# Weight sums in one list at a higher rate, and the down product's first quarter sums begun when their tile is written

## The chip, the cores and the metric

The kernel runs on one core of a Trainium2 chip. The metric is the device time of one execution in microseconds (us); lower is better. Each kernel is timed in several runs and the median is told. One execution is also recorded by the profiler. All data are float32.

## The reference

The input is 2048 tokens of 512 features. A first layer (time mixing and channel mixing as in RWKV) and a gated feed-forward layer are added to it, one after the other:

```
h = layer_norm(layernorm(x));  hh = time_shift(h)
k, v, r = three 512x512 products of mixtures of h and hh
x1 = layernorm(x) + (sigmoid(r) * wkv(k, v)) @ Wo.T
kv = silu(mix(ln(x1)) @ Wkey.T) @ Wval.T          # 512 -> 2048 -> 512
x  = x + x1 + sigmoid(mix(ln(x1)) @ Wcr.T) * kv
gate, up = split(layernorm(x) @ w_gate_up.T)      # 512 -> 2 x 2048
out = x + (silu(gate) * up) @ w_down.T            # 2048 -> 512
```

## The kernel before

**Tiling.** The tokens are cut into four blocks of 512 (`NB` = 4). The first half of the program takes all blocks through the first layer, the second half takes them through the feed-forward layer. Each 512x512 product is done in seven products of 256x256 quarters instead of eight (Strassen in Winograd's form). That needs sums of quarters on both sides. The sums of activations (`sums_of`, line 435) are made block by block on VectorE. The sums of weights don't depend on a block: each is made once, stored in DRAM scratch, and then loaded like a weight.

**Weight sums** (`prepare`, line 140). One job loads four quarters on GpSimd's DMA queue into `raw` tiles, forms four sums on VectorE (128x512, line 155) and stores each on GpSimd's queue. The jobs are in a queue, `preps`. The first nine are pushed at the start. `WK, WR, WV, WO` follow before the loop over blocks. The last nineteen, the list `late`, are the feed-forward layer's: eight for gate and up, and eleven for the down product, four of them (`d`) feeding three later ones (`dd`). They are pushed within block 1, after `up_unit(1, 0)`. A job can begin only when it is pushed; with depth 1, the next begins when the one ahead has ended.

**Pacing.** After each product, `tick` (line 287) adds `credit[1]` to a credit, and as long as a planner's slack of VectorE time is positive, a step of the head job may be taken for one credit (`prep_one`). A step goes ahead of the background work (norms, mixes). After a job's loads, five ticks pass before its first sum (`WAIT`). `credit[1]` is 0.5 until the nineteen are pushed, then 0.42. What is left at the end of the first half is forced out in one go, before the first half's pools are given back:

```python
1283    while preps:
1284        need_sums(preps[-1][0])
1285    mixes.close()
1286    last_room()
```

PE, VectorE and ScalarE run their instructions in the order in which this code issues them.

**Down product** (`down_product`, line 1075). In the second half, the product with `w_down` goes down one level more: each of the seven products (`DOWN`, line 1037) is again seven products of 128x128 quarters, its steps `first` to `seventh`. The quarter sums of the activation tile, four VectorE instructions into `quads` tiles (`quarter_sums`, line 1064), are asked for per product n. For n = 0 (tile `B11`) and n = 1 (tile `B22`) this is done in `done` of the last up unit (line 1020), behind the four sums of the hidden tile itself. `done` is put off by two ticks. For n > 1 they are asked for when product n - 2 ends. If the third product of n finds its sums not asked for, it runs the put-off functions, then all urgent work ahead of them (`product`, line 1118). The two last products of the up unit (`held`) are interleaved with the first steps of n = 0. For blocks 0 to 2 the next block's gate unit is computed between the up unit and the down product; the last block has none.

Of the kernel before, what the change touches and what calls it, by code (L numbers as in the profile page):

```python
# [33 lines left out]
WK, WV, WR, WO, WCR = range(5)  # L34
# [15 lines left out]
B11, B12, B21, B22, T1, T2, T4 = range(7)  # L50
# [8 lines left out]
def rwkv_ffn_kernel(  # L59
# [80 lines left out]
    def prepare(n, own):  # L140

        raw = []
        for k in range(4):
            t = prep.tile([P, 2, HB], F32, tag="raw", name="raw") if own else q_tile("q")
            paced(nc.gpsimd.dma_start(flat(t), sources[n][k]))
            raw.append(t)
        yield 1
        a11, a12, a22, a21 = raw
        for k, o, i0, i1, op in (
            (0, a22, a21, a22, ALU.add),  # L150
            (2, a21, a11, a21, ALU.subtract),
            (1, a11, a22, a11, ALU.subtract),
            (3, a12, a12, a11, ALU.subtract),
        ):
            tt(o, i0, i1, op)
            nc.gpsimd.dma_start(sums[n][k], flat(o))  # L156
            yield
# [24 lines left out]
    def load_x(b, queues=None):  # L182
        t = tok_tile("x")
        for k in range(NT):
            eng = queues[k] if queues else nc.sync
            paced(eng.dma_start(t[:, k, :], x_t[b][:, k, :]))
        return t
# [55 lines left out]
    credit = [0.0, 0.0]  # L243
# [17 lines left out]
    def begin(item):  # L261
        if not item[4]:
            item[4] = True
            next(item[2])
            item[1] = WAIT

    def prepare_all(ns, own, depth):
        empty = not preps
        for n in ns:
            preps.append([n, 0, prepare(n, own), depth, False])  # L270
        if empty:
            for item in list(preps)[:depth]:
                begin(item)
# [31 lines left out]
    def push(name, gen, ready=None):  # L305
        background.append([ready, gen, name, False, background])

    def urgent(name, gen):
        hot.append([None, gen, name, False, hot])

    def need(name):
        while name not in finished:
            run_one(True)
        slack[0] = min(slack[0], 0.0)
        spent[0] = 0.0
# [46 lines left out]
    def tt(out, a, b, op):  # L362
        nc.vector.tensor_tensor(out, a, b, op)  # L363
        cost(size(out))
# [70 lines left out]
    def sums_of(B):  # L435

        for o, i0, i1 in (T1, B12, B11), (T2, B22, T1), (T4, B21, T2), (T3, B22, B12):
            tt(B[o], B[i0], B[i1], ALU.subtract)
            yield
# [272 lines left out]
    def time_norm(b):  # L712
        xb = xin.pop(b)
        mv = small.tile([P, NT, 2], F32, tag="mv", name="mv")
        yield from moments(xb, mv)
        var = small.tile([P, 2 * NT], F32, tag="var2", name="var2")
        affine(var, mv)
        two = small.tile([P, 2 * NT], F32, tag="two", name="two")
        yield from rsqrt(var, two, 2 * NT)
        rstd, both = two[:, :NT], two[:, NT:]  # L720
        h = tok_tile("h")
        yield from scaled(xb, h, mv, both)
        hT = htp.tile([P, NC, TB + 1], F32, tag="hT", name="hT_a")
        hTs[b, "a"] = hT
        tails[b] = residual(b, xb, [(mv[:, t, 0:1], rstd[:, t : t + 1]) for t in range(NT)])
        yield 1
        yield from shifted_norm("a", h, hT, LN1G, LN1B)
# [89 lines left out]
    def time_mix(b, name):  # L817
        row = {"k": MK, "r": MR, "v": MV}[name]
        yield from mix((b, name), hTs[b, "a"], row, b < PLAIN)

    def push_mix(b, name, gen):
        norm = f"normb{b}" if name in ("cr", "ck") else f"norm{b}"
        push((b, name, "t"), gen, lambda: norm in finished and op_free())
# [42 lines left out]
    def v_unit(b):  # L866
        q = qs[b]

        def sink(i, j, c):
            tt(q[i, j], c, q[i, j], ALU.mult)  # L870

        def done():
            hidden_sums((b, "g"), q, b < PLAIN)

        product_of(b, WV, "v", sink, False, done)
# [4 lines left out]
    def out_unit(b):  # L880
        need(("x1", b))

        def sink(i, j, c):
            v = block_view(x1s[b], i, j)
            tt(v, c, v, ALU.add)

        product_of(b, WO, "g", sink, True, free=None)
# [20 lines left out]
    def channel_mix(b, name):  # L908
        yield from mix((b, name), hTs[b, "b"], {"cr": CR, "ck": CK}[name])

    def gate_unit(b):
        def sink(i, j, c):
            s = q_tile("sr")
            nc.scalar.activation(s, c, AF.Tanh, scale=0.5)  # L914
            gates[b, i, j] = s

        product_of(b, WCR, "cr", sink, True)

    def up_unit(b, g):
        s = {}  # L920

        def sink(i, j, c):
            t = q_tile("s")
            nc.scalar.activation(t, c, AF.Silu)
            s[i, j] = t

        unit(
            [WKEY + g],
            [Lazy((b, "ck"))],
            sink,  # L930
            False,
            lambda: hidden_sums((b, g), s),
            op_done if g == 3 else None,
        )
# [27 lines left out]
    def load_resid(b):  # L962
        r = tok_tile("resid")
        paced(nc.sync.dma_start(r, resid[b]))
        loads[b] = r, load_x(b)
# [42 lines left out]
    def ffn_up(b, g):  # L1008
        s = gated.pop((b, g))
        hid = hidden.setdefault(b, {})  # L1010

        def sink(i, j, c):
            q = (B11, B12, B21, B22)[2 * i + j]
            if q not in hid:
                hid[q] = hidden_tile()
            tt(hid[q][:, g], c, s[i, j], ALU.mult)
            if g == 3:
                made.add((b, q))

        def done():  # L1020
            if g == 0:
                for t in (T1, T2, T4):
                    hid[t] = hidden_tile()
            urgent((b, "f", g), sums_of({t: hid[t][:, g] for t in hid}))
            if g == 3:
                made.update((b, t) for t in (T1, T2, T4, "T3"))
                for n in range(2):
                    quarter_sums(b, n)

        unit([WU + g], [Lazy((b, "z"))], sink, False, done, op_done if g == 3 else None)  # L1030

# [7 lines left out]
    def hidden_tile():  # L1039
        return room["hidden"].tile([P, 4, 2, HB], F32, tag="hid", name="hid")  # L1040
# [15 lines left out]
    def quarter_operand(b, n):  # L1056

        x = quarters(hidden[b][DOWN[n][1]])
        new = room["sets"][n % 2]
        x[T1], x[T2], x[T4] = new[:3]  # L1060
        x["T3"] = new[3] if n < 2 else x[B12]
        return x

    def quarter_sums(b, n):
        x = quarter_operand(b, n)
        asked.add((b, n))

        def run():
            for o, i0, i1 in (T1, B12, B11), (T2, B22, T1), (T4, B21, T2), ("T3", B22, B12):
                tt(x[o], x[i0], x[i1], ALU.subtract)  # L1070
                yield

        urgent((b, "quarters", n), run())
# [144 lines left out]
    late = [n + g for g in range(4) for n in (WG, WU)] + [("dd", A11)]  # L1218
# [25 lines left out]
    push_mix(0, "ck", channel_mix(0, "ck"))  # L1244
    r_unit(1)
    v_unit(1)
    prepare_all((WK, WR, WV, WO), True, 1)
    for b in range(NB):
        nxt = b + 2 < NB
        if nxt:  # L1250
            xin[b + 2] = load_x(b + 2)
        if b == NB - 1:
            load_resid(0)
        gate_unit(b)
        if b + 1 < NB:
            out_unit(b + 1)
        need((b, "ck"))
        if nxt:
            push(f"norm{b + 2}", time_norm(b + 2))
        for g in range(4):  # L1260
            up_unit(b, g)
            if b == 1 and g == 0:
                prepare_all(late, True, 1)
                credit[1] = 0.42
            if g == 0:
                if nxt:
                    push_mix(b + 2, "k", time_mix(b + 2, "k"))
                    push_residual(b + 2)
                    push_mix(b + 2, "r", time_mix(b + 2, "r"))
                if b + 1 < NB:  # L1270
                    push(f"normb{b + 1}", channel_norm(b + 1))
                if nxt:
                    push_mix(b + 2, "v", time_mix(b + 2, "v"))
                if b + 1 < NB:
                    push_mix(b + 1, "cr", channel_mix(b + 1, "cr"))
                    push_mix(b + 1, "ck", channel_mix(b + 1, "ck"))
        if b == NB - 1:
            push((0, "z", "t"), ffn_in(0), op_free)
        down_unit(b)
        if nxt:  # L1280
            for n, u in (("k", k_unit), ("r", r_unit), ("v", v_unit)):
                u(b + 2)
# [90 lines left out]
```

## Time and profile before

| | |
|---|---|
| median of 3 runs | 1298.44 us (1295.93 to 1301.96) |
| the profiled execution's own time | 1300.73 us |
| its span, first to last instruction | 1298.6 us, so 2.1 us lie around it |
| PE matmuls | 1245.6 us busy (96% of the span) |
| PE weight loads | 1114.2 us (86%), beside the matmuls |
| VectorE (DVE) | 777.6 us (60%) |
| ScalarE (ACT) | 368.5 us (28%) |
| GpSimd (POOL) | 151.4 us (12%) |
| DMA | 288.55 MB, mean 222 GB/s |
| mean granted TensorE clock | 0.984 |

In the profile, a line such as L527 is the kernel's source line. L527 is the matmul of the seven-product units, L640 that of the plain units, L1126 that of the down product, L414 a transpose. L363 is every VectorE two-input operation, so the tile names tell them apart: `raw` is a weight sum, `quads` a quarter sum, `hid<-hid` a sum of the hidden tile, `u` and `s` a combination of products. L145 and L156 are the loads and stores of a weight sum. A float32 matmul has two records.

### The profile page before, as it was taken

Reading aid. Unit: us, or ns where it says so; the run is one execution under the profiler, and the core shown is the slowest. Engines: PE = TensorE matmul, PEld = TensorE weight load, DVE = VectorE, ACT = ScalarE, POOL = GpSimd, SP = SyncE. Lnnn points to the kernel's source line nnn. Section 1 sums busy time; section 2 is a strip of 40 time slices with the busy share of each in tenths; the row PEclk is TensorE's granted clock in tenths of the full one; section 3 lists DMA queues with packets and bytes.
Section 4 is the critical chain, followed back from the end, with each engine's and each line's share of the span. In section 5 each row is a group of like instructions: output and inputs, shape, how many; then the busy total and the mean of one; then the engine's idle time right before and its main releaser. Section 6 shows DMA issues by size and latency. Waiting matters only on the chain.

```text
span 1298.6 us, 18324 instructions
## 1 busy us (share of the span) xinstructions
PE 1245.6 (96%) x6572; PEld 1114.2 (86%) x6572; DVE 777.6 (60%) x1416; ACT 368.5 (28%) x687; POOL 151.4 (12%) x276
## 2 busy tenths in 40 slices
PE   9999999999999999999992999999999999999988
PEld 7888888878888788888881788998889988998878
DVE  4757587576774767544743365665756564663456
ACT  5533352343522424113100223212221222112211
POOL 2222221200111111121213000000000000000000
PEclk9999999999999999999996899999999999999989
DMA  5666777865778777788777654795459854785556
GB/s 191 223 211 235 238 237 256 289 197 180 231 221 257 240 231 238 243 305 284 239 240 266 212 153 146 219 330 190 146 163 295 280 154 145 240 280 154 154 172 202
DMA packets 137960, 288.55 MB, mean 222 GB/s; under 512 B 17296, under 2 KB 18320, under 8 KB 136848
## 3 DMA queue, kind: packets, MB, share of 16 engines
q1 hardware_dynamic: 115424, 215.53, 53.3%
q0 software_dynamic: 21440, 70.27, 15.1%
q10 hardware_dynamic: 1008, 1.59, 0.3%
q8 instruction: 53, 0.87, 0.3%
q14 instruction: 35, 0.29, 0.1%
HBM read 245.39 MB, written 41.94 MB: 221 GB/s over the span
## 4 chain that ended last, share of the span: by engine, by line
PE 89%; DVE 3%; ACT 3%; DMA 2%; issue 2%; POOL 1%; POOLq 0%; DVEq 0%
PE ps L527 68%; PE ps L1126 13%; PE ps L640 6%; PE ps L414 1%; DMA dd<-raw 1%; DMA raw<-in_wd 1%; DVE u L363 1%; ACT mix L465 1%; DVE hid L363 1%; POOL dd L156 0%; ACT r L835 0%; DVE quads L363 0%; DMA raw<-d 0%; DMA x<-in_x 0%; ACT e L840 0%
## 5 line engine op out<-in xcount | busy, mean ns | idle before, releaser
L527 PE MATMUL ps<-zT,w 128*128 128x256 f32 x1792 | 393.7, 381 | 28.5 <-ACT u L544 28.5
L527 PEld LDWEIGHTS ps<-zT,w 128*128 128x128 f32 x1792 | 340.0, 191 | 74.9 <-ACT u L544 28.9
L527 PE MATMUL ps<-mix,w 128*128 128x256 f32 x1232 | 273.5, 381 | 5.3 <-ACT s L544 5.3
L527 PEld LDWEIGHTS ps<-mix,w 128*128 128x128 f32 x1232 | 234.8, 191 | 38.3 <-ACT s L544 6.1
L363 DVE TENSOR_TENSOR u<-ps,u 128x512 f32<-128x512 f32 x128 | 88.5, 691 | 167.2 <-PE ps L527 164.9
L544 ACT COPY u<-ps 128x512 f32<-128x512 f32 x128 | 74.8, 584 | 327.0 <-PE ps L527 327.0
L527 PE MATMUL ps<-w,s 128*128 128x256 f32 x512 | 114.3, 379 | 0.0
L527 PEld LDWEIGHTS ps<-w,s 128*128 128x128 f32 x512 | 97.0, 190 | 13.0
L1126 PE MATMUL ps<-w,hid 128*128 128x128 f32 x832 | 105.9, 277 | 0.4 <-ACT r L1138 0.4
L1126 PEld LDWEIGHTS ps<-w,hid 128*128 128x128 f32 x832 | 100.8, 194 | 1.1 <-ACT r L1138 0.5
L1126 PE MATMUL ps<-w,quads 128*128 128x128 f32 x704 | 91.6, 280 | 8.2 <-issue 5.5
L527 PE MATMUL ps<-w,t 128*128 128x256 f32 x432 | 96.3, 379 | 1.7 <-ACT sr L914 1.2
L1126 PEld LDWEIGHTS ps<-w,quads 128*128 128x128 f32 x704 | 85.6, 195 | 10.7 <-issue 5.9
L527 PEld LDWEIGHTS ps<-w,t 128*128 128x128 f32 x432 | 81.9, 190 | 13.5 <-ACT sr L914 1.6
L363 DVE TENSOR_TENSOR raw<-raw 128x512 f32<-128x512 f32 x92 | 63.2, 687 | 45.1 <-DMA raw<-in_wd 20.4
L640 PE MATMUL ps<-mix,w 128*128 128x256 f32 x384 | 85.5, 385 | 1.1 <-DVE mix L371 1.1
L640 PEld LDWEIGHTS ps<-mix,w 128*128 128x128 f32 x384 | 73.7, 193 | 11.6 <-DVE mix L371 1.5
L363 DVE TENSOR_TENSOR s<-ps,s 128x512 f32<-128x512 f32 x64 | 44.1, 690 | 59.5 <-PE ps L527 45.7
L363 DVE TENSOR_TENSOR u<-u,u 128x512 f32<-128x512 f32 x64 | 44.1, 689 | 59.4 <-ACT u L544 59.4
L1138 ACT COPY r<-ps 128x128 f32<-128x128 f32 x112 | 29.7, 265 | 151.2 <-PE ps L1126 151.2
L1208 POOL DMA_DIRECT2D out<-resid x12 | 8.6, 717 | 440.8 <-DVE resid L363 440.8
L363 DVE TENSOR_TENSOR hid<-hid 128x512 f32<-128x512 f32 x84 | 56.6, 687 | 1.1
(127 smaller groups left out, 1177.7 us busy)
## 6 DMA issues: line engine op xcount, KB each, us to landing
w<-sum SPq DMA_DIRECT2D x304, 256.0 KB, 3.2
w<-in_w SPq DMA_DIRECT2D x256, 256.0 KB, 3.3
w<-dd SPq DMA_DIRECT2D x112, 256.0 KB, 3.6
raw<-in_w POOLq DMA_DIRECT2D x48, 256.0 KB, 4.8
sum<-raw POOLq DMA_DIRECT2D x48, 256.0 KB, 3.9
w<-d SPq DMA_DIRECT2D x48, 256.0 KB, 3.4
q<-in_w POOLq DMA_DIRECT2D x36, 256.0 KB, 5.4
sum<-q POOLq DMA_DIRECT2D x36, 256.0 KB, 3.5
```

Of the source, the lines that this page charges most:

```text
L363: nc.vector.tensor_tensor(out, a, b, op)
L414: nc.tensor.transpose(flat[:, t * P : (t + 1) * P], h[:, t, c * P : (c + 1) * P], ident)
L465: nc.scalar.activation(dst(c), hT[:, c, 0:TB].rearrange("p (j t) -> p j t", j=2), AF.Copy, scale=onem[:, row - MK, c : c + 1],)
L527: mm = nc.tensor.matmul(pz[:, m, :], lhsT=lhsT, rhs=rhs, start=first and g == 0 and m == 0 and k == 0, stop=g == last and k == 1, skip_gro ...
L544: nc.scalar.copy(tmp[name], acc["z"])
L640: mm = nc.tensor.matmul(acc[i, j][:, m, :], lhsT=act[:, k, lo] if by_token else wg[:, k, lo], rhs=wg[:, k, :] if by_token else act[:, k, : ...
L1126: mm = nc.tensor.matmul(dst, lhsT=x[k][:, g, :], rhs=wt[:, g, :], start=first and g == 0, stop=g == 3, skip_group_check=True,)
L1138: nc.scalar.copy(st["r"][:, m, n * P : (n + 1) * P], st["z"])
L1208: eng.dma_start(out_t[b][:, 2 * j : 2 * j + 2, i * HB : (i + 1) * HB], rs[b][:, 2 * j : 2 * j + 2, i * HB : (i + 1) * HB],)
```

## The change

The nineteen late jobs join the list of four before the loop, so that they can begin as soon as those four have ended. The rate after `up_unit(1, 0)` becomes 0.55 in place of 0.42. The quarter sums for n = 0 and n = 1 are asked for as soon as the last up unit has written that tile's last quarter (`B11`, `B22`), no longer in `done`.

```diff
@@ ffn_up, sink
             if g == 3:
                 made.add((b, q))
+                if q in (B11, B22):
+                    quarter_sums(b, 0 if q == B11 else 1)
@@ ffn_up, done
                 made.update((b, t) for t in (T1, T2, T4, "T3"))
-                for n in range(2):
-                    quarter_sums(b, n)
@@
-    prepare_all((WK, WR, WV, WO), True, 1)
+    prepare_all([WK, WR, WV, WO] + late, True, 1)
@@
             up_unit(b, g)
             if b == 1 and g == 0:
-                prepare_all(late, True, 1)
-                credit[1] = 0.42
+                credit[1] = 0.55
```

## The prediction

> **What bounds the kernel now.** I read the page's first two parts, then PE's waits, then the chain of waits and the timeline around the two longest, then windows. On the page PE is busy in nearly every fortieth of the span, 1245.6 of 1298.6 us. So TensorE sets the time, and what can be won is its idle time and its time at a lowered clock.
>
> ```profile
> PE   9999999999999999999992999999999999999988
> ...
> PEclk9999999999999999999996899999999999999989
> ```
>
> Slice 22 of 40 is the exception: PE at 2 tenths, then a lowered clock. The last slices are short too. PE's waits name them (us in total, times, longest):
>
> ```profile
> PE ps L527 <- ACT u L544: 28.5, 1, 28.5
> PE ps L1126 <- issue: 5.5, 1, 5.5
> PE ps L527 <- ACT s L544: 5.3, 2, 3.0
> PE ps L1126 <- DVE quads L363: 2.0, 3, 0.7
> ```
>
> One wait of 28.5 us is more than half of all idle time. It is put down to a ScalarE copy, but the chain shows what that copy stood behind (start, us, what):
>
> ```profile
> 684.86 8.61 DMA dd<-raw
> ...
> 699.04 4.05 DMA raw<-d
> ...
> 707.52 4.85 DMA raw<-in_wd x2
> ...
> 712.45 0.70 DVE raw L363
> ...
> 715.24 0.69 DVE s L363
> 715.95 0.63 ACT s L1003
> 716.58 0.48 ACT u L544
> 717.11 62.96 PE ps L527 x281
> ```
>
> These are the last weight sums, forced out by line 1284. VectorE's first combination of the second half (`s`) stands behind them, ScalarE behind that, PE behind ScalarE. The 5.5 us wait is in the last block's down product (start, us):
>
> ```profile
> 1243.77 2.74 DVE L363 TENSOR_TENSOR hid<-hid 128x512 f32<-128x512 f32 x4
> 1246.42 0.68 DVE L363 TENSOR_TENSOR quads<-hid 128x512 f32<-128x512 f32 x1
> 1247.14 1.42 DVE L363 TENSOR_TENSOR quads<-hid,quads 128x512 f32<-128x512 f32 x2
> ...
> 1247.93 2.05 PE L1126 MATMUL ps<-w,quads 128*128 128x128 f32 x8 [5.54 <-issue]
> ```
>
> PE is done at 1242.4. The third product of n = 0 needs `quads`, and VectorE makes them only after the add of 1242.43, one `hid` and four sums of `hid`. The three waits of 0.67 us on `quads` (825.7, 969.4, 1113.1) are the same place in blocks 0 to 2, where another unit covers most of it.
>
> **Part 1, the wait between the halves.** The changed program has the same instructions; only their order differs. In VectorE's order before, fourteen weight sums stand directly ahead of that first combination. After, the last weight sum stands ahead of the four `zT` sums and fifteen more instructions. Those `zT` sums ran at 655.4, and PE reached the seam at 681.5. So the jobs end some 26 us before they would hold anything up. **Gain 28.5.** Next late: PE did four products from 681.52 to 688.6, and the fifth needs the `u` copy. In the timeline that is add at about 685 (0.69), `s` on ScalarE (0.63), copy (0.57), the copy no earlier than the third product's end at about 686.9: done by 687.5, ahead of 688.6. The new pools' memory was last read by the down product's `sr` operations (to 683.9 on VectorE, same queue). SP issues the same list in the same order; the residual's load behind the store of 684.20 (median 9.1 us to landing) could hold it until 693.3, with weights loaded ahead. I take 0 for the seam, upper end 3.
>
> The clock: between 688.6 and 717 the granted clock falls to 0.59, is 0.50 to 720 and 0.87 to 725. 98 weight loads then took 23.24 us; at the pace before the stall (32 records in 6.91 us from 660.80 to 667.71, 0.216 each) they take 21.2. **Gain 2.1.** The Trainium skill, "TensorE: Matmul & The Clock Gate", What's actually happening, says that the clock halves after an idle window of about 3.4 us and returns after as long a busy one. An estimate by it is 1.7 us lost at each of the two long stalls, and the sum below would be 1.5 smaller. The trace agrees on the half clock but not on the threshold: 2.31 us of idling at 270 brought 0.50, 2.97 us at 436 left 1.00.
>
> **Part 2, quarter sums.** In the last block `B11` is whole at 1230.86 and VectorE then idles until 1235.27 (4.42 us): room for four sums (2.8). The third product then starts at 1242.4. **Gain 5.5.** Next late is n = 1: its four sums follow `B22` (whole at 1240.34) and end near 1243.2; its third product comes six products of 0.89 us after 1242.4, at 1247.8. They delay the add of 1242.43, hence `hid` and its sums, to 1247.3; `T2`, second of those, is ready at 1245.9 and needed near 1251. The sums of n = 2 start near 1249.0, `T2`'s quarter is out at 1250.4 and needed near 1255. No wait is left by this count, with 3 to 5 us of cover each. If none of it came, 8.3 would be lost to me. The clock again: five products took 1247.93 to 1255.24, 7.3 us, at 0.50 to 0.71; at 0.89 (1255.24 to 1257.92, three products) they take 4.5. **Gain 2.8.** Blocks 0 to 2: 0.67 on `quads` and 0.28 on the copy behind them, 0.95 each. **Gain 2.9.**
>
> **Part 3, what the jobs do where they go.** No DMA or sum is added. GpSimd's 28 issues and VectorE's 16 sums of 674 to 717 are spread forward. The row for `raw` in windows by time (DVE busy, POOL busy, clock, DMA share, GB/s):
>
> ```profile
> 255.00:307.00 52.00, 2.74 (x4) 2.17 (x4) 0.97 0.63 200
> 307.00:674.00 367.00, 41.19 (x60) 67.38 (x124) 1.00 0.77 246
> 674.00:717.00 43.00, 11.06 (x16) 15.23 (x28) 0.73 0.76 266
> ```
>
> After, 76 sums (52.2 us) lie in about 270 to 655, 0.136 of VectorE in place of 0.112; VectorE as a whole was busy 225.4 of 367. The eight that fall into 255 to 307 bring it from 35.2 to about 40 of 52. GpSimd's transfers go from 88 to 104 GB/s, so DMA from 246 to about 261, share 0.82. PE never waited on a weight in the trace, and the same loads lead by the same ring of 12. Both loads fit on average; what counts is places where PE waits on VectorE. At 296.78 PE waited 0.50 for a `t` sum; in the new order `t`'s first sum no longer runs ahead of the add before it: +0.7. At 436.44 it waited 2.97 behind, among others, two of `mix` (1.42 together) that now follow instead: -1.6 with the gap between them. The 2.31 at 270 is ahead of any difference and stays. Take a gain of 0.9; bounds: the rest of the 2.97 gone too (gain 2.3), or one landing wait of a load at such a place (the longest in the trace was 6.7, most of it covered; loss 3).
>
> **The sum.** 28.5 + 2.1 + 5.5 + 2.8 + 2.9 + 0.9 = 42.7. From the profiled execution, 1300.73 - 42.7 = 1258.0. It lies 2.3 above the median, so by the median 1255.7; I say **1256**.
>
> **Rivals.**
> 1. *Another wait takes the seam* (residual load, pool memory, a late copy). 3 us beyond the count and the clock loss kept (2.1): near 1261. Against it: every other releaser there is done by 688. 0.08.
> 2. *The last block's stall only moves*, since one VectorE queue does `hid` sums, eight quarter sums and `r` adds between 1240 and 1252: 5.5 + 2.8 stay, 1264. For it: VectorE is busy without a break in 1242 to 1248. Against: the cover counted above. 0.08.
> 3. *Slower: the forced wait is paid in nineteen pieces.* A job's first sum stands in VectorE's queue whether or not its loads have landed; PE's adds queue behind. In 255 to 670 it waited so for 6.67, 4.37 and 3.62 us, with no PE wait; the two longer were in block 2's down product, where VectorE has little to do. In single-weight units a product is 1.72 us and about two are ahead: 6.67 each time would idle PE 3.2 us, 19 times 61, and the time 1317. It decides from 42.7 / 19 = 2.2 us per job, that is a landing wait of 5.7 in every job. Against: loads land in 4.2 us (median, 8.4 at most), five ticks are 8.6, the 3.62 fell among single-weight units and was covered, and the other waits put down to such a load are at most 1.33 (one of 5.57 has no named releaser). [...] 0.04.
> 4. *The same in part*: about 1 us at each job, 1256 + 19 = 1275. 0.06.
> That the change doesn't do what it says is excluded for part 1 by the order; for part 2 it is rival 2.
>
> **How the numbers follow.** The forecast holds 0.74. Its own range is 1255.7 less 2.3 and 2.5 (lowest run shown against the median), and plus 3.9 and 3.5 (highest): 1251 to 1263. With rivals 1 and 2 the range is **1250 to 1268**; it leaves out 3 and 4. About 0.5% (6.5 us) is what a measurement of this kernel can tell from no change. All cases but 3 are faster by more than that: faster 0.95, same 0.01, slower 0.04.
>
> **What would show it.** PE's wait `<- ACT u L544` of 28.5 gone, no `raw` operation after the `zT` sums, PEclk without the 6 and 8; the `quads` of the last block near 1231 less the shift, the 5.5 and three 0.67 gone; PE's idle sum near 15 in place of 53. Wrong if PE waits on `u`, `s` or `mix` whose VectorE queue shows a wait on `DMA raw`, or if a wait on weights (`DMA w`) appears.

## The result, and the profile after

The changed kernel takes **1258.24 us** (median of 4 runs, 1257.87 to 1260.03) beside 1299.22 us for the kernel before in the same rounds (1295.93 to 1301.96): ratio **0.9688, 95% interval 0.9663 to 0.9713**. In five more rounds it took 1257.19 (1256.22 to 1260.08) beside 1299.59: ratio 0.9681 (0.9666 to 0.9697). The forecast was 1256.

The profiled execution took 1260.03 us, its span is 1258.2. First the page, the same two rows as before (40 slices in tenths):

```profile
PE   9999999999999999999999999999999999999998
...
PEclk9999999999999999999999999999999999999999
```

The slice with a 2 is gone, and so are the 6 and the 8 of the clock. PE is busy 1240.0 of 1258.2 us, so it idles 18.2 us where it idled 53.0; the prediction had said near 15. The largest of PE's waits that are left (us in total, times, longest):

```profile
PE ps L527 <- ACT s L544: 6.0, 3, 2.3
PE ps L527 <- issue: 1.8, 1, 1.8
```

The waits of 28.5 on `u`, of 5.5 in the last down product and the three on `quads` are not there any more. But `<- ACT s L544` has grown from two waits to three: one of them the prediction did not have.

The timeline at the seam between the halves (start, us, engine, line):

```profile
683.97 46.35 PE L527 MATMUL ps<-zT,w 128*128 128x256 f32 x214
```

That is 214 matmul records in a row without a gap. VectorE's queue in front of it:

```profile
653.70 0.68 DVE L363 TENSOR_TENSOR raw<-raw 128x512 f32<-128x512 f32 x1
658.06 0.69 DVE L363 TENSOR_TENSOR zT<-zT 128x512 f32<-128x512 f32 x1 [3.69 <-ACT zT L987]
...
687.70 0.69 DVE L363 TENSOR_TENSOR s<-ps,s 128x512 f32<-128x512 f32 x1 [1.38 <-PE ps L527]
```

The last weight sum ends at 654.4, ahead of the `zT` sums and 29.6 us before PE reaches the seam. The first combination `s` now waits for PE, no longer PE for it. The `u` copy follows from 689.35 to 689.93, and PE's fifth product would need it at about 691.0 (683.97 and four products of 1.77).

The last block's down product, VectorE first, then PE:

```profile
1199.06 0.69 DVE L363 TENSOR_TENSOR quads<-hid 128x512 f32<-128x512 f32 x1
...
1201.12 0.68 DVE L363 TENSOR_TENSOR quads<-hid 128x512 f32<-128x512 f32 x1
...
1212.55 2.74 DVE L363 TENSOR_TENSOR hid<-hid 128x512 f32<-128x512 f32 x4
```

```profile
1210.40 1.05 PE L1126 MATMUL ps<-w,quads 128*128 128x128 f32 x8
```

The four quarter sums of n = 0 end at 1201.8, in VectorE's gap, and no longer behind the four sums of `hid`. The third product starts on time at 1210.40, right behind the one ahead of it, and the next ones follow every 0.89 us (1211.30, 1212.19, 1213.08), the pace that the kernel before has only from 1254.35 on.

**Where the 40.4 us of span went.** The same marks are read from both timelines: PE's start after its first wait in the first half (270.15 before, 268.29 after), its arrival at the seam (681.52, 683.97), the first L1126 product of block 0 (819.42, 791.05) and of block 3 (1236.73, 1204.90), and the first of the two waits on `r` near the end (1291.50, 1251.12).

| stretch | before | after | gain | predicted |
|---|---|---|---|---|
| start to the first mark | 270.15 | 268.29 | 1.86 | 0 |
| to the seam | 411.37 | 415.68 | -4.31 | 0.9 |
| seam to block 0's down product | 137.90 | 107.08 | 30.82 | 30.6 |
| to block 3's down product | 417.31 | 413.85 | 3.46 | 2.9 |
| to the mark before the end | 54.77 | 46.22 | 8.55 | 8.3 |
| rest | 7.10 | 7.08 | 0.02 | 0 |

Everything behind the seam came as predicted, to 1.1 us in 42. The first half did not. The 1.86 at the start are not the change's, which alters nothing so early: the granted clock of the first 20 us was 0.91 in the one execution and 1.00 in the other.

**The first half.** PE's waits in the first half after the change (end of each row: idle time before it, and its releaser):

```profile
268.29 8.86 PE L527 MATMUL ps<-mix,w 128*128 128x256 f32 x32 [2.31 <-ACT s L544]
295.64 1.96 PE L527 MATMUL ps<-w,t 128*128 128x256 f32 x8 [1.23 <-ACT sr L914]
434.27 7.17 PE L527 MATMUL ps<-mix,w 128*128 128x256 f32 x32 [1.67 <-ACT s L544]
460.55 1.97 PE L527 MATMUL ps<-w,t 128*128 128x256 f32 x8 [1.83 <-issue]
512.95 8.86 PE L527 MATMUL ps<-mix,w 128*128 128x256 f32 x32 [2.06 <-ACT s L544]
```

Before, these places had 2.31, 0.50, 2.97, 1.23 and nothing. So +0.7 and -1.3 are the two terms that the prediction had (+0.7, -1.6); +0.6 near 460 and 2.1 at 512.95 were not in it. The last is paid twice: its 32 records take 8.86 us in place of 7.17, since the granted clock is 0.65 from 512.9 to 517. That adds 1.7. Together that is a loss of 3.8; some 0.5 of the 4.3 is not placed.

What releases PE at 512.95 stands in ScalarE's queue:

```profile
505.35 2.55 ACT L465 ACTIVATE mix<-hT_b,onem 128x512 f32<-128x512 f32 x4
...
507.80 0.56 ACT L544 COPY u<-ps 128x512 f32<-128x512 f32 x1
508.26 1.33 ACT L465 ACTIVATE mix<-hT_b,onem 128x512 f32<-128x512 f32 x2
...
512.33 0.57 ACT L544 COPY s<-ps 128x512 f32<-128x512 f32 x1
```

Four `mix` operations stand ahead of a copy out of PSUM (`ps` in the rows, where the matmuls write), and two more, with their VectorE halves, ahead of the combination that the last copy waits for. Before, the same place looked like this:

```profile
506.91 1.32 ACT L465 ACTIVATE mix<-hT_b,onem 128x512 f32<-128x512 f32 x2
508.14 0.56 ACT L544 COPY u<-ps 128x512 f32<-128x512 f32 x1
```

There, four `mix` had run earlier, from 502.66 to 505.2, and ScalarE idled for 1.16 after them. Two stand directly ahead of the copy, and none between it and the next copy (511.49). They are block 3's channel mixes, background work that the planner deals out. After the change they come later, and so does the end of the transposes that they follow: before, PE makes this block's 16 transpose records in one go at 493.27, after it 12 at 491.70 and the last 4 only at 501.65. The change touches no line of all this; it only gave other ticks to the weight sums.

### The profile page after: what moved, and what is told of

It is laid out like the page before. It is cut to its first block, busy times and chain, and to the rows that moved or that the text cites. A ratio compares the mean times of both kernels' runs of the same rounds, so it can differ in the third digit from the quotient of the medians.

```text
span 1258.2 us, 18321 instructions
## 1 busy us (share of the span) xinstructions
PE 1240.0 (99%) x6572; PEld 1110.7 (88%) x6572; DVE 777.4 (62%) x1416; ACT 369.0 (29%) x687; POOL 151.3 (12%) x276
## 4 chain that ended last, share of the span: by engine, by line
PE 93%; ACT 3%; DVE 2%; DMA 1%; issue 1%; POOL 0%; DVEq 0%
PE ps L527 71%; PE ps L1126 14%; PE ps L640 6%; PE ps L414 2%; ACT mix L465 1%; DMA raw<-in_w 1%; DVE u L363 0%; DMA w<-in_w 0%; DVE mix L371 0%; DMA x<-in_x 0%; ACT r L835 0%; ACT e L840 0%; DVE e L371 0%; ACT x L701 0%; ACT mix L782 0%
## 5 line engine op out<-in xcount | busy, mean ns | idle before, releaser
L544 ACT COPY u<-ps 128x512 f32<-128x512 f32 x128 | 74.8, 584 | 319.4 <-PE ps L527 319.4
L527 PEld LDWEIGHTS ps<-w,s 128*128 128x128 f32 x512 | 97.0, 190 | 13.1
L1126 PE MATMUL ps<-w,hid 128*128 128x128 f32 x832 | 104.7, 275 | 0.4 <-ACT r L1138 0.4
L1126 PEld LDWEIGHTS ps<-w,hid 128*128 128x128 f32 x832 | 99.5, 192 | 1.1 <-ACT r L1138 0.5
L1126 PE MATMUL ps<-w,quads 128*128 128x128 f32 x704 | 89.5, 276 | 0.4 <-ACT r L1138 0.4
L1126 PEld LDWEIGHTS ps<-w,quads 128*128 128x128 f32 x704 | 84.3, 192 | 1.1 <-ACT r L1138 0.5
L1138 ACT COPY r<-ps 128x128 f32<-128x128 f32 x112 | 29.6, 264 | 142.7 <-PE ps L1126 142.7
```

The source lines that it names most:

```text
L527: mm = nc.tensor.matmul(pz[:, m, :], lhsT=lhsT, rhs=rhs, start=first and g == 0 and m == 0 and k == 0, stop=g == last and k == 1, skip_gro ...
L544: nc.scalar.copy(tmp[name], acc["z"])
L1126: mm = nc.tensor.matmul(dst, lhsT=x[k][:, g, :], rhs=wt[:, g, :], start=first and g == 0, stop=g == 3, skip_group_check=True,)
L1138: nc.scalar.copy(st["r"][:, m, n * P : (n + 1) * P], st["z"])
```

## The experiments

Twelve more runs were made, each beside the kernel before; nine repeats the changed kernel, and ten repeats seven. The theory: the gain is the two removed waits with their clock, they are independent, and the nineteen jobs cost almost nothing where they now lie. Diffs are against the changed kernel.

### One: the list alone

```diff
@@ ffn_up, sink
-                if q in (B11, B22):
-                    quarter_sums(b, 0 if q == B11 else 1)
@@ ffn_up, done
+                for n in range(2):
+                    quarter_sums(b, n)
```

> The list joined at rate 0.55, the quarter sums asked for as before, behind the hidden tile's own sums. My theory (the two parts add up): the wait of 28.5 us between the halves stays gone, and the three waits of 0.67 on quads and the 5.5 us wait of the last block are back, with the lowered clock behind the latter: 1258.2 + 2.9 + 8.3 = 1269.4 us. Rival (the early quarter sums are hidden anyway, and the gain in the down product comes from VectorE being less behind): about 1258 to 1261 us.

Measured: 1271.07 (1267.73 to 1273.05), ratio 0.9768 (0.9748 to 0.9788). The two waits are back, to the digit:

```profile
PE ps L1126 <- issue: 5.5, 1, 5.5
PE ps L1126 <- DVE quads L363: 2.0, 3, 0.7
```

### Two: the quarter sums alone

```diff
-    prepare_all([WK, WR, WV, WO] + late, True, 1)
+    prepare_all((WK, WR, WV, WO), True, 1)
@@
-                credit[1] = 0.55
+                prepare_all(late, True, 1)
+                credit[1] = 0.42
```

> The early quarter sums alone, weight sums as before (late list pushed in block 1, rate 0.42). My theory: 1299.2 - 11.2 = 1288.0 us, with the wait of 28.5 us between the halves unchanged. Rival (quarter sums hidden anyway): 1299 us, the 5.5 us wait having moved to a later product of the last block.

Measured: 1287.03 (1286.37 to 1288.95), ratio 0.9901 (0.9887 to 0.9916), and only the seam's wait is left of the three:

```profile
PE ps L527 <- ACT u L544: 28.2, 1, 28.2
```

So the parts add up: 29.0 (1300.09 - 1271.07) and 13.1 (1300.09 - 1287.03) are 42.1, both together 41.0 to 42.4 in the two measurements. Neither part hides or feeds the other.

### Three, four and five: how many sums are left at the seam

Is the seam's wait a matter of the number of sums left, or of when their loads were issued? Three kernels leave some. The first keeps the list joined at the old rate:

```diff
-                credit[1] = 0.55
+                credit[1] = 0.42
```

> As the changed kernel, but at the old rate 0.42 after block 1's first up unit: the pause alone is removed. In VectorE's order eight weight sums (two jobs) are then left directly ahead of the second half's first combination, in place of fourteen before and none after. My theory (the wait is the chain of loads, sums and stores of the jobs left, about 8.5 us a job, less what PE has ahead): a wait of 12 to 17 us and 2 us of lowered clock, so 1271 to 1277 us. Rival (joining the list is enough, the rate does nothing): 1258 us.

Measured: 1273.12 (1271.36 to 1273.37), ratio 0.9789 (0.9775 to 0.9804). Eight sums are left, PE waits 12.8. The second keeps the pause and takes the higher rate:

```diff
-    prepare_all([WK, WR, WV, WO] + late, True, 1)
+    prepare_all([WK, WR, WV, WO], True, 1)
@@
             if b == 1 and g == 0:
+                prepare_all(late, True, 1)
                 credit[1] = 0.55
```

> As the changed kernel, but the late list is pushed in block 1 as before, with the rate 0.55: the rate alone is raised. Four weight sums (one job) are left directly ahead of the second half's first combination. My theory: a wait of 4 to 8 us there and up to 2 us of lowered clock, so 1263 to 1268 us. Rival (the rate is enough, the pause does nothing): 1258 us.

Measured: 1262.13 (1261.51 to 1263.13), ratio 0.9708 (0.9694 to 0.9723). Four sums are left and PE waits 2.4. The third holds the last job (`("dd", A22)`) back until the first half has been issued:

```diff
-    late += [...] + [("dd", q) for q in (S4, S2, A12, S1, S3, A22)]
+    late += [...] + [("dd", q) for q in (S4, S2, A12, S1, S3)]
@@
+    prepare_all([("dd", A22)], True, 1)
     while preps:
```

> As the changed kernel, but the last job of the list is pushed only when the first half has ended, so that its loads, four sums and stores are forced out between the halves. As with the raised rate alone, four sums stand directly ahead of the second half's first combination; there, the loads had been issued earlier and the wait was 2.4 us. My theory (the wait is set by when the last job's loads are issued, not by how many sums stand there): loads issued near 683 to 685 land near 690, four sums of 0.69, then add, silu and copy (2 us) give a wait of 4.5 to 7 us and 1 to 2 us of lowered clock: 1264 to 1267 us. Rival (number of sums): 2.4 us, 1260 to 1261 us.

Measured: 1269.05 (1267.3 to 1272.71), ratio 0.9769 (0.9752 to 0.9785): above what either theory gave. Four sums again, yet PE waits 7.2, three times as long. The timelines of the second and of the third kernel say why:

```profile
679.79 2.17 POOL L145 DMA_DIRECT2D raw<-in_wd  x4
687.59 2.87 DVE L363 TENSOR_TENSOR raw<-raw 128x512 f32<-128x512 f32 x4 [2.46 <-DMA raw<-in_wd]
```

```profile
686.70 2.17 POOL L145 DMA_DIRECT2D raw<-in_wd  x4 [45.95 <-PE ps L527]
695.82 2.87 DVE L363 TENSOR_TENSOR raw<-raw 128x512 f32<-128x512 f32 x4 [7.24 <-DMA raw<-in_wd]
```

In the one the loads are issued at 679.79 and VectorE waits 2.46 for them; in the other at 686.70, and it waits 7.24. The sums themselves take 2.87 in both. PE reaches the seam at 682.78 in the one and at 686.24 in the other, so the loads go out 3.0 us ahead of it and 0.5 behind it. Run twelve, further down, lies between: it leaves four sums too, their loads go out at 685.54, 1.3 ahead of its seam (686.80), and PE waits 4.6. In run three, the last two loads go out only at 691.49 and 692.39, behind the stores of the job ahead. So what a leftover job costs is set mainly by when its last loads go out, not by its sums: four sums cost 2.4, 4.6 or 7.2; eight cost 12.8, and fourteen 28.5. In run five, the profile's span (1271.0) is 12.8 us longer than the changed kernel's: 7.2 are the wait, 3.3 more lie behind it ahead of block 0's down product, and 2.0 are in the first half, where PE waits 2.90 near 461 in place of 1.83 and its next 8 records take 3.35 in place of 1.97.

### Six: the nineteen jobs left out

This kernel leaves out the late jobs' loads, sums and stores; plain weight quarters are loaded in the place of their sums.

```diff
@@ weight
+        if q >= 4 and n >= WG:
+            return ring(sources[n][q - 4])
@@ down_weight, likewise for "dd" and "d"
-            need_sums(("dd", q))
-            src = sums["dd", q][k - 4]
+            src = wd[min(q, 3), k - 4]
@@
-    prepare_all([WK, WR, WV, WO] + late, True, 1)
+    prepare_all([WK, WR, WV, WO], True, 1)
```

> The changed kernel without the nineteen late jobs: no loads, sums or stores for them, and the feed-forward layer loads plain quarters where it would load a sum (so its products differ; the number of loads and matmuls is the same). It bounds what the jobs cost where they now lie. My theory (PE-bound, the jobs cost only the places where VectorE or ScalarE's order delays PE, 0.7 at 296, 0.6 at 460, 3.9 at 513): 1252 to 1256 us. Rival (they cost by load on VectorE and DMA, spread over the first half): 1240 to 1248 us.

Measured: 1255.28 (1253.41 to 1256.7), ratio 0.9666 (0.9652 to 0.9681). So 76 loads, 76 sums and 76 stores cost 1.9 to 3.0 us by the medians of two measurements of the changed kernel, with intervals that overlap this one's. By the timeline it is 3.1: the first half without them takes 410.75, with them 412.12 in the execution of run nine, where one stretch of lowered clock (1.7) less is paid. Nearly all of their transfers and VectorE time is absorbed, and the rival by which the jobs are the next large cost falls. Of the 3.1, 2.1 are the wait of 512.95, which this kernel doesn't have. It is the cost of one order against another: the wait near 434 is 2.97 here and 1.50 in run nine, those near 296 and 460 are 0.50 each here, and 1.23 and 1.83 there.

### Seven and ten: the channel mixes later

If block 3's `mix` operations ahead of the copy make the wait of 512.95, it goes when they are pushed after block 2's last up unit.

```diff
             if g == 0:
...
-                if b + 1 < NB:
-                    push_mix(b + 1, "cr", channel_mix(b + 1, "cr"))
-                    push_mix(b + 1, "ck", channel_mix(b + 1, "ck"))
+            if b + 1 < NB and g == (3 if b + 1 == NB - 1 else 0):
+                push_mix(b + 1, "cr", channel_mix(b + 1, "cr"))
+                push_mix(b + 1, "ck", channel_mix(b + 1, "ck"))
```

> The changed kernel with one thing moved: the channel mixes of block 3 are pushed after block 2's last up unit in place of its first. PE's new wait of 2.06 us at 513 stood behind four mix operations in ScalarE's queue ahead of the copy that PE needs; here they come after that copy. My theory (the burst of mix makes the wait, and the lowered clock after it costs 1.8): both go, 1258.2 - 3.9 = 1254.3 us. Rival (the wait comes from VectorE being fuller and reappears at the next combination): 1257 to 1260 us.

Measured: 1255.97 (1255.57 to 1258.08), ratio 0.9676 (0.9661 to 0.969). The wait and the clock behind it are gone; two of the three waits on `s` are left, and those near 296 and 460 stay as well:

```profile
PE ps L527 <- ACT s L544: 3.6, 2, 2.3
```

Nine and ten are the changed kernel and this one again, on one chip in the same five rounds.

> The changed kernel once more, beside the next three and in more rounds. Expected 1258 (1257 to 1260) and the same waits as in its first profile: 2.31 near 268, 1.23 near 296, 1.67 near 434, 1.83 near 461, 2.06 near 513. If the lowered clock behind the wait of 513 is a matter of chance, it can be there or not; that is worth 1.8 us.

> Block 3's channel mixes issued later, once more, beside the changed kernel of the same chip and rounds. If the 2.06 us wait of 513 and the clock behind it cost the changed kernel what its timeline says, this one is 2.1 to 3.9 us below it (1254 to 1256); if the first run's 2.3 us were scatter, the two are within 1 us.

Measured: nine 1257.19 (1256.22 to 1260.08), ratio 0.9681 (0.9666 to 0.9697); ten 1256.03 (1255.59 to 1258.08), ratio 0.9672 (0.9658 to 0.9685). So the cause of the wait is shown, since it goes with the mixes, twice. That this version is faster is not: 1.2 and 2.3 us by the medians, with intervals that overlap. Run nine shows one reason. Its profile has all five waits and no lowered clock behind any:

```profile
268.19 7.17 PE L527 MATMUL ps<-mix,w 128*128 128x256 f32 x32 [2.31 <-ACT s L544]
...
510.97 7.17 PE L527 MATMUL ps<-mix,w 128*128 128x256 f32 x32 [2.06 <-ACT s L544]
```

The same program idles the same 2.31 and 2.06, and 32 records take 7.17 where they took 8.86. Twice 1.7 is 3.4 of the 3.6 us between its span (1254.6) and that of the first profile (1258.2).

### Eight, eleven and twelve: the rate, and sums behind urgent work

Eight sums are left at 0.42 and none at 0.55; the rates between 0.50 and 0.55 issue the same program, so a rate just below them was taken.

```diff
-                credit[1] = 0.55
+                credit[1] = 0.48
```

> The changed kernel at rate 0.48 (any rate from 0.50 to 0.55 gives the same program). Four weight sums come after the zT sums, the last two just ahead of the down product's last combination but none behind it. My theory (sums cost nothing until they stand ahead of the second half's first combination late): 1257 to 1260 us, no wait between the halves, the 513 wait still there since the four mix stand at the same place. Rival (each sum moved later costs): 1261 us or more.

Measured: 1266.2 (1263.6 to 1267.66), ratio 0.9749 (0.9734 to 0.9764). I had expected 1260 at most; it is 6 us above that. The seam is free, but the first half is slower: this profile reaches its wait near 521 at 521.23, run nine its own at 510.97. Of these 10.3 us, 1.8 are there at the first mark (its first 20 us ran at a granted clock of 0.91, those of run nine at 1.00), 3.5 are more waiting, and most of the rest is lowered clock behind the waits. PE's longest wait in the first half, and VectorE's queue ahead of it, from the timelines of the two engines:

```profile
467.80 2.96 PE L527 MATMUL ps<-w,t 128*128 128x256 f32 x8 [3.76 <-issue]
```

```profile
459.00 2.14 DVE L363 TENSOR_TENSOR mix<-mix 128x512 f32<-128x512 f32 x3
...
464.96 1.41 DVE L363 TENSOR_TENSOR raw<-raw 128x512 f32<-128x512 f32 x2
466.29 0.68 DVE L363 TENSOR_TENSOR t<-e 128x512 f32<-128x512 f32 x1
```

Two weight sums stand ahead of the `t` sums that PE's next product reads. No landing is waited for here. In the changed kernel one stands there (458.43), and PE waits 1.83 (460.55). So two more kernels let weight sums give way:

```diff
@@ tick
-            if preps and credit[0] >= 1 and prep_one():
+            if preps and not hot and credit[0] >= 1 and prep_one():
```

Eleven has this and the late mixes at 0.55, twelve this alone at 0.48.

> Late mixes, and a weight sum is taken in a tick only when no urgent work (the t sums of a product, hid sums, quarter sums) is open. If the waits near 296 and 461 come from weight sums that stand ahead of the t sums in VectorE's queue, they go back to 0.5 and 1.2 or less: 1.4 us gained, 1253 to 1255. Rival: the sums that give way come later in a heap and put a landing wait or four sums in front of something else, at the end of the first half above all: 1256 to 1262.

> Rate 0.48 with the same rule that weight sums give way to urgent work. In the run at 0.48 without the rule PE waited 3.76 near 468 with two weight sums ahead of the t sums. If their place is the cause, no wait of over 2 us stands near 468 here; if it is the landing of loads or something else, it stays. The whole time is not the test: with this rule four or more sums are left behind the zT sums, which cost 2 to 7 us in the runs that left four. 1258 to 1268.

Measured: eleven 1256.62 (1255.73 to 1257.76), ratio 0.9674 (0.9661 to 0.9688); twelve 1266.38 (1265.4 to 1270.56), ratio 0.9754 (0.9737 to 0.9772). With no sum ahead of `t`, PE's wait at that place is 1.23 in both (460.24 and 463.37). So 0, 1 and 2 sums ahead go with 1.23, 1.83 and 3.76: one step is a sum's 0.6, and of the second step, 1.9, another 0.7. The other 1.2 are not the weight sums': in eight, three `mix` operations (459.00, shown above) stand ahead of the `u` sum of 461.05, which starts 1.6 after the end of the copy that it reads (459.48), where in the changed kernel it starts 0.3 after it (454.45, 454.16). This is read from the timelines; no run tests it by itself. As an improvement the rule gave nothing: in eleven the wait near 268 grew from 2.31 to 2.97 and that near 296 stayed at 1.23, so the 0.5 that I expected there was wrong. Why the latter didn't go was not found. In twelve four sums are left over (693.82), and PE waits 4.6 at the seam.

## Why the prediction was right, and where it was off

**The seam's wait (28.5): right.** The order of VectorE's queue decided it, and that could be read without a run. Run two, with the list undone, has it back at 28.2; three, four and five leave less of it, by what they leave over and when it was loaded. Next late was named right too: the `u` copy was counted to end 1.1 ahead of PE's need (687.5 against 688.6) and ended 1.1 ahead (689.9 against 691.0). Neither residual load nor pool memory held PE. Rival 1 falls.

**The clock at the seam (2.1): right.** From the seam to block 0's down product it is 137.90 before, or 109.38 without the wait of 28.52, and 107.08 after: 2.3 behind the wait where 2.1 were said.

**The last block (5.5 and 2.8): right.** 8.55 was measured, that is 5.54 of waiting and 3.0 behind it. Run one has the same 5.54 again. The moved stall of rival 2 does not appear: n = 1's sums (`quads` at 1208.55) push the four `hid` sums behind the add of 1211.22, and no product waits for them.

**Blocks 0 to 2 (3 times 0.95): slightly low.** From one down product to the next it is 143.72 before and 142.56 after, 1.16 each. The 0.2 more per block lie in two products that I didn't count: in block 0, those of 825.70 and 827.84 take 1.00 in place of 0.89 until the next one starts.

**The first half (gain 0.9): the step that failed.** The two places that I had looked at came out (+0.7 and -1.3). What failed is that I looked only where PE already waited. An order dealt out by credits and slack shifts all the background work when the jobs shift, on ScalarE too, and a place without a wait can get one. That happened at 512.95 (2.06, and 1.7 of clock) and near 460 (0.6). The loads on the engines came as counted (from 270 to 655 DMA moves 260 GB/s at a share of 0.80, where I had said 261 and 0.82), but they did not decide it. The true figure is a loss of 4.3 in the first profile; with no lowered clock in either program (411.37 less 1.69 before, 412.12 in run nine) it is 2.4. The lower bound that I gave for this step, a loss of 3 by one landing wait, had about the size but not the mechanism: background operations in ScalarE's queue, not a load, as run seven shows.

**The sum.** 42.7 was predicted. The profiled execution gives 40.4 and the medians 41.0 and 42.4. The 1.9 us at the start of before's profile, which are not the change's, and 1.05 more behind the seam than predicted hid part of the first half, which came out 5.2 worse than I had said; that the sum came so near is in part luck. By the medians I was 1.5 to 2.5 low, from 1255.7. The lower end of my range was also reckoned wrongly: of the 2.3 that I took off, 0.9 was in the sum already, so 1.4 should have gone off, and the forecast's own range would begin at 1252 in place of 1251.

**Rival 3 (slower, 1317): falls, with its condition.** It was to decide from 2.2 us per job. Run six gives 3.1 / 19, or 0.16. VectorE did wait for landings between 255 and 690, but in five places only, once for 1.0 us on `raw<-in_wd` and four times as follows (us in total, times, longest):

```profile
DVE raw L363 <- DMA raw<-d: 4.5, 2, 3.3
DVE raw L363 <- DMA raw<-in_w: 4.4, 2, 2.4
```

These five come to 9.9 us, where before had 16.2, and fell beside PE work that was already queued; only the 1.67 at 434 came soon after one (1.99, ended at 428.4), and it is less than before's 2.97. The issue of the loads isn't held up either: GpSimd issues four in 2.17 us, 0.54 each, fifteen times between 300 and 660, with two-input operations of VectorE beside them (at 440.02) as without (at 544.55), and just so at 686.70 in run five, where VectorE waits. Rival 4 (1 us per job) falls with the same number.

## What to carry to other kernels

Work that is forced out at a phase's end stands in an in-order queue ahead of the next phase, and what it costs is set by when its last loads go out, more than by its own operations. Begin it early enough that the last load is issued well before the phase ends, and check ahead of which operations it then stands. When a planner deals out work, moving one kind moves all: compare the whole order of every engine against the places where the bounding engine has little lead, not only where it waits already. An early start of a small sum, in a gap that the queue has anyway, is worth the whole wait and the clock behind it.

## What the runs showed of the hardware

A short idle time of TensorE is often paid twice, and one program does both: run nine and the first run of the changed kernel idle the same 2.31 and 2.06 us, with the lowered clock behind them in one execution and not in the other. Of the 26 places in all fourteen profiles where PE idled 2.06 to 2.97 us in the first half ahead of 32 records of products of `mix`, 20 had the clock lowered behind them, by the time of the records (most 8.86 us for the 32, three 8.57 to 8.81), and 6 had not (7.17). It was 4 of 6 after 2.06, 12 of 14 after 2.3 and 4 of 6 after 2.97, so the length within this span doesn't decide it; behind 1.26 to 1.67 us (nine places) the 32 records always took 7.17. Ahead of products of `t`, 2.10, 2.90 and 3.76 us (runs one, five and eight) had the clock lowered too (8 records in 3.50, 3.35 and 2.96 us in place of 1.97), and 1.83 us, six times, had not. The Trainium skill, "TensorE: Matmul & The Clock Gate", What's actually happening, puts the idle window at about 3.4 us. The half clock is as it says; the threshold isn't, since 2.06 us can be enough here and 2.97 us can leave the clock up. What else enters, the runs don't show.
